# A transformer block and a ConvNeXt block on one core: q and k computed in pairs of tiles with seven block products instead of eight

## The chip, the core and the metric

The program runs on one core of a Trainium2 chip. The core has five engines, each with its own queue of instructions that are begun in order: TensorE (PE in the profile; PEld is its weight load) multiplies matrices into PSUM, VectorE (DVE) and ScalarE (ACT) work element by element, GpSimd (POOL) and SyncE (SP) are used here to start transfers. Engines wait for each other through semaphores. The metric is the time of one execution on the device in microseconds (us), as a median of several executions.

## The reference, cut to what matters

The input x is eight images of 384 channels by 32x32 pixels, in float32. Two layers follow each other: attention with an MLP, and a 7x7 depthwise convolution with an MLP that has a global response norm. In the kernel every 128x128 block of weights times 512 pixels is one TensorE product.

```python
# layer 0 (per image: N = 1024 tokens, C = 384 channels, 8 heads of 48)
xn  = layernorm(xf, g1, beta1)
qkv = einsum('bnc,oc->bno', xn, w_qkv) + b_qkv          # q, k, v
attn = softmax(einsum('bhnd,bhmd->bhnm', q, k) * SCALE)
out = einsum('bhnm,bhmd->bhnd', attn, v)
x1  = einsum('bnc,oc->bno', out, w_proj) + b_proj + xf
h   = gelu(einsum('bnc,oc->bno', layernorm(x1, g2, beta2), w_fc1) + b_fc1)
y   = x1 + einsum('bnh,oh->bno', h, w_fc2) + b_fc2
# layer 1
z = layernorm(depthwise_conv7x7(y) + dw_b) * ln_w + ln_b
z = gelu(einsum('bhwc,cd->bhwd', z, w1) + b1)
z = grn_gamma * (z * nx) + grn_beta + z                 # nx: over all pixels of an image
out = y + einsum('bhwd,dc->bhwc', z, w2) + b2
```

## The kernel before: the parts that the change and the prediction touch

The kernel is software-pipelined over the images. While TensorE works on one image's attention and MLP, VectorE does the convolution of the image before it. In the steady part TensorE's order per image is: w1 (of the image before the last), v of the new image, w2, q/k, attention, proj, fc1, fc2.

A small clock in the program, `flow`, decides where side work is placed in the order of instructions. It counts the time of the TensorE products already recorded, and a side chain says with `yield us` after how much of it the next piece is to be recorded.

```python
U = 0.857                       # one 128x128x512 product, for the clock
ps_s = ...tile_pool(name="ps_s", bufs=2, space=PSUM)    # [P, 1024] each: two banks
ps_o = ...tile_pool(name="ps_o", bufs=4, space=PSUM)    # [P, 512] each: one bank
ring = ...tile_pool(name="ring", bufs=9)                # weights, loaded up to 9 tiles ahead

def qk(b, xn):                  # q and k of one image: six output tiles m, i
    big = one.tile([P, HT * N], F32, tag="big", name=f"qk_{b}")
    parts = big[:, : 2 * NP * N].rearrange("p (i m n) -> p i m n", i=2, m=NP)
    for m in range(CT):                                 # CT = 3
        for i in range(2):                              # q, k
            ...
            def evict(dst, ps):
                nc.scalar.activation(dst, ps, AF.Identity, bias=bqk[:, at : at + 1], scale=1.0 if i else SCALE)
            args = lambda k: wqk_sb[:, k, at, :], lambda k: xn[:, k, :], CT
            if (m, i) != (CT - 1, 1):
                evict(parts[:, i, m, :], linear(*args, f"qk_{b}_{at}"))   # 3 x 2 products
    ...
    def last_tile():            # the sixth tile, called behind the first two score tiles
        for h in range(2):
            evict(parts[:, 1, CT - 1, half(h)], linear_half(*args, h, f"qk_{b}_last_{h}"))
        ...

# attention: 64 steps; each has one score tile, one exp, and the product of two steps before
for n in range(len(steps) + 2):
    if n == 2:
        last_tile()
    if n < len(steps):
        ps[n] = scores(*steps[n])         # PE s, then nc.scalar.activation(p, s, AF.Exp)
    if n >= 2:
        product(*steps[n - 2], ps.pop(n - 2))           # PE o
    ...
```

The MLP of layer 1 (w1) already uses the scheme that the change brings to q/k. Two output tiles (rows) and the first two input tiles are a 2x2 block of weights, the two halves of the pixels a 2x2 block of input, and seven products with sums of blocks take the place of eight; the third input tile takes four more, plainly. The sums of weights (s1 to s4) are made once, the differences of inputs (t1 to t4) per image by `block_differences`, in the buffer `attn`.

```python
def block_differences(acc):
    ...
    yield 3.0
    for dst, one_, other in ((t1, b12, b11), (t2, b22, t1), (t3, b22, b12), (t4, b21, t2)):
        nc.vector.tensor_tensor(dst, one_, other, ALU.subtract)
        yield 1.2

def grn_up(...):                # w1, for each of six pairs
            nc.scalar.copy(c21, product((a11, b11)))
            ...
            plus(c11, product((a13, b31), (a12, b21)), c21)    # plus: a VectorE addition, L982
            accumulate(p5, [(s1, t1)])
            plus(c21, product((s2, t2)), c21)
            plus(c12, p5, c21)
            plus(c12, product((s4, b22), (a13, b32)), c12)
            ...
            plus(c21, product((s3, t3)), c21)
            plus(c22, p5, c21)
            plus(c21, product((a23, b31), (a22, t4)), c21)
            plus(c22, product((a23, b32)), c22)
```

w2 (`o_p` in the profile, `kept` is its result) ends with two VectorE operations on its last product:

```python
    p = product(d)
    op(c11, p, c11)             # L787 kept<-o_p
    done(0, 0)
    op(c21, p, c21)             # L787 kept<-o_p
    done(1, 0)
```

The convolution is 49 taps for each of three channel tiles. VectorE does 42 of them (L911, `acc<-pad,vec,acc`), ScalarE multiplies for the other seven in halves (L932, `tap`) and GpSimd's queue adds those by transfers (L933). In the last image what is left of the convolution is recorded at once before the last convolution begins (`wqkv<-pad,vec,wqkv`).

```python
def convolution(acc, us, slow=0, ...):
    ...
            yield 2.43 if n <= CT * slow else us

start_conv(b, 1.65)             # image 0
start_conv(b, 1.8, 10)          # other images: 30 taps every 2.43 us, then every 1.8 us

def next_values(b):
    if b < B:
        flow.finish(state["norm1"])
        values(b, state["xn"])  # v
```

Of the kernel before, what the change touches and what calls it, by code (L numbers as in the profile page):

```python
# [46 lines left out]
F32 = mybir.dt.float32  # L47
AF = mybir.ActivationFunctionType
ALU = mybir.AluOpType
# [102 lines left out]
def block_kernel(  # L152
# [26 lines left out]
    quiet = []  # L179
    s_fc2 = dram.tile([P, len(FORMS), 4 * P], F32, tag="s_fc2", bufs=1, name="s_fc2")  # L180
    s_w2 = dram.tile([P, len(FORMS), 4 * P], F32, tag="s_w2", bufs=1, name="s_w2")
    s_w1 = dram.tile([P, HT // 2, 4, P], F32, tag="s_w1", bufs=1, name="s_w1")

    def half(h):
# [121 lines left out]
    def plan_thirds(name, w, sums):  # L306
        plan = []
        for i, form in enumerate(FORMS):
            plain = form[0] == "a"
            plan.append(((name, i), block_of(w, int(form[1]), int(form[2])) if plain else sums[:, i, :]))  # L310
        return plan

    def plan_fc2_fast(tag):
        return plan_thirds(f"fc2_{tag}", wfc2, s_fc2)

    def plan_w1(tag, fast=True):
        plan = []
# [169 lines left out]
            other = 64 * (i % 2) + HD  # L487
            yield at(NP - 1)[own : own + 16], at(i // 2)[other : other + 16]

    def qk(b, xn):  # L490

        big = one.tile([P, HT * N], F32, tag="big", name=f"qk_{b}")
        parts = big[:, : 2 * NP * N].rearrange("p (i m n) -> p i m n", i=2, m=NP)
        for m in range(CT):
            for i in range(2):
                at = i * CT + m

                def evict(dst, ps):
                    nc.scalar.activation(dst, ps, AF.Identity, bias=bqk[:, at : at + 1], scale=1.0 if i else SCALE)  # L499

                args = lambda k: wqk_sb[:, k, at, :], lambda k: xn[:, k, :], CT
                if (m, i) != (CT - 1, 1):
                    evict(parts[:, i, m, :], linear(*args, f"qk_{b}_{at}"))
        moves = [(own, other) for i in range(2) for own, other in pieces(lambda m: parts[:, i, m, :])]
        for own, other in moves[:-2]:
            nc.sync.dma_start(out=own, in_=other)

        def last_tile():

            for h in range(2):  # L510
                evict(parts[:, 1, CT - 1, half(h)], linear_half(*args, h, f"qk_{b}_last_{h}"))
            for own, other in moves[-2:]:
                nc.sync.dma_start(out=own, in_=other)

        return parts[:, 0], parts[:, 1], last_tile

    def heads(t):
# [369 lines left out]
        nc.sync.dma_start(out=kept.rearrange("(c p) n -> p c n", p=P), in_=xt)  # L887
        return kept

    def convolution(acc, us, slow=0, y0=0, y1=H, ready=tuple(range(CT)), taken=None):  # L890

        done = [0] * CT
        ct, n = None, 0
        taps = KS * KS - (HELPED if taken is not None else 0)
        while min(done) < taps:
            left = [c for c in ready if done[c] < taps and not (taken and taken.get(c, 0) > flow.now)]
            if not left:
                yield 1.0  # L900
                continue
            ct = min([c for c in left if c != ct] or left, key=lambda c: done[c])
            i = done[ct]
            dy, dx = divmod(i, KS)
            window = pad[:, ct, dy + y0 : dy + y1, dx : dx + W]
            dst = image(acc[:, ct, :])[:, y0:y1, :]
            tap = col("dww", ct * KS * KS + i)
            if i == 0:
                nc.vector.tensor_scalar(dst, window, tap, col("dwb", ct), ALU.mult, ALU.add)
            else:  # L910
                nc.vector.scalar_tensor_tensor(dst, window, tap, dst, ALU.mult, ALU.add)  # L911
            done[ct] += 1
            n += 1
            yield 2.43 if n <= CT * slow else us

    def help_convolution(acc, us, taken):

# [274 lines left out]
    def prepare(weights, aside):  # L1192
# [120 lines left out]
        if aside:  # L1313
            yield from shift_through_w1()
            return
        yield from forms("fc2", wfc2, s_fc2)
        weights.release()
        t = blocks("w1_sums")
        tiles = w1.rearrange("p (i a o) -> p i a o", a=6, o=P)
# [22 lines left out]
    def main():  # L1342
# [14 lines left out]
        nc.gpsimd.memset(high, 1.0)  # L1357
        make_identity(nc, ident)
        xt = load_x(0, "x", engine=nc.gpsimd)
        plan = plan_fc1(0) + plan_fc2_fast(0)  # L1360
        for b in range(1, B):
            if b < B - 1:
                plan += plan_fc1(b) + plan_fc2_fast(b)
            else:
                for h in range(2):
                    plan += plan_fc1(f"{b}_{h}") + plan_fc2(f"{b}_{h}")
            plan += plan_w1(b - 1, b < B - 1)
            if b == B - 1:
                plan += plan_w1(f"{b}_0", False)
            plan += plan_w2(b - 1, b < B - 1)  # L1370
        plan += plan_w1(f"{B - 1}_1", False) + plan_w1(f"{B - 1}_2", False)
        plan += plan_w2(f"{B - 2}_b", False)[4:] + plan_w2(B - 1, False)
        weights = Weights(plan, "fc2_0")
# [10 lines left out]
        state = {"help": None, "xn": xn, "conv": None, "acc": None, "norm1": None, "norm3": None}  # L1384
        kept = {}

        def start_conv(b, us, slow=0):
            acc = state["acc"] = one.tile([P, CT, N], F32, tag="acc", name=f"acc_{b}")
            taken = {}
            state["conv"] = flow.spawn(convolution(acc, us, slow, taken=taken), paced=True)  # L1390
            state["help"] = flow.spawn(help_convolution(acc, 2.7, taken), paced=True)

        def conv_norm(b, ln):
# [21 lines left out]
        def next_values(b):  # L1415

            if b < B:
                flow.finish(state["norm1"])
                values(b, state["xn"])

# [7 lines left out]
        def last_convolution(h, ct, ln=None):  # L1430
            if ct < 0:
                conv_norm(B - 1, ln)
                next_norms(B - 1)
                return
            ready[h].append(ct)
            if ct == 0:
                rows = (LAST[0].stop // W, H) if h else (0, LAST[0].stop // W)
                conv = convolution(last, 0.86 if h else 0.66, 0, *rows, ready[h])
                state["conv"] = flow.spawn(after(state["conv"], conv), paced=True)
                if h == 0:  # L1440
                    state["norm_a"] = flow.spawn(after(state["conv"], last_norm(LAST[0], 2.6)))

        for b in range(B):
            if b == 0:
                folding = flow.spawn(after(None, folds(weights), 8))
                preparing = flow.spawn(after(None, prepare(weights, False), 4))
                aside = flow.spawn(after(folding, prepare(weights, True), 4))
            qT, kT, last_tile = qk(b, state["xn"])
            ln2, rest, xn = attention(b, xt, qT, kT, last_tile, (folding, aside) if b == 0 else ())
            if b < B - 1:  # L1450
                mlp(b, xt, xn, weights, b, ln2, rest, lambda: next_norms(b), lambda ln: conv_norm(b, ln))
            else:
                acc = state["acc"]
                mlp_by_halves(b, xt, xn, weights, ln2, rest, last_convolution)
            kept[b] = keep(b, xt)
            if b + 1 < B:
                acc = state["acc"]
            if b == 0:
                xt = load_x(b + 1, "x")
                flow.finish(preparing)  # L1460
                start_conv(b, 1.65)
                next_values(1)
                continue
            if b < B - 1:
                xt = load_kept(b - 1, kept.pop(b - 1))
            flow.finish(state["norm3"])
            if b < B - 1:
                y, gx = grn_up(b - 1, acc, weights, b - 1)
                start_conv(b, 1.8, 10)
                scale = flow.spawn(grn_scale(b - 1, gx, weights, b - 1, y))  # L1470
                next_values(b + 1)
                flow.finish(scale)
                quiet.append("w2")
                grn_down(b - 1, y, xt, weights, b - 1, b - 1)
                quiet.clear()
                xt = load_x(b + 1, "x")
            else:

                norm_b = flow.spawn(after(state["conv"], last_norm(LAST[1], 1.0)))
                norm_c = flow.spawn(after(norm_b, last_norm(LAST[2], 1.2)))  # L1480
                y, gx = grn_up_straight(b - 1, acc, weights, b - 1)
                scale = flow.spawn(grn_scale(b - 1, gx, weights, b - 1))
                flow.finish(state["norm_a"])
                sums = small.tile([P, CT, HT], F32, tag="gx_last", bufs=1, name="gx_last")
                y_last = places()
                last_up(last, y_last, 0, sums, weights)
                flow.finish(scale)
                halves = lambda k, part: y[:, k, part]
                blocks = [(r, half(n)) for r in range(CT) for n in range(2)]
                args = b - 1, halves, kept[b - 1], weights  # L1490
                grn_down_straight(*args, b - 1, b - 1, blocks[:-1])
# [147 lines left out]
```

## Time and profile before

| what | value |
|---|---|
| time, median of three | 3334.23 us (3333.64 to 3336.33) |
| span of the profiled execution | 3332.5 us, granted TensorE clock 0.996 |
| one image in the steady part | 403.5 to 404.1 us |
| VectorE busy in such an image | 303 us |
| ScalarE busy in such an image | 202 us |
| TensorE busy, all | 3298.9 us |
| q/k products: `qk` and `qk_last`, records | 480 and 96 |

The page of the profile gives the busy time of each engine, and the costliest groups of instructions as line, engine, operation, output<-input, shape and count, with the busy time and the mean of one in ns. A float32 matmul has two records, each with a weight load. The chain of waits follows the work that ended last, as start, duration and what; its counts include weight loads. The timeline has start, duration, engine, line and operation, with the idle time ahead of it and what ended it in brackets.

### The profile page before, as it was taken

The numbers are of one execution on the slowest core, as the hardware profiler recorded it, in microseconds if no ns is written. First come the engines' busy times: TensorE is split into PE (matmuls) and PEld (weight loads), VectorE is DVE, ScalarE is ACT, GpSimd is POOL, SyncE is SP. The second block draws the span as 40 slices with busy tenths as digits, with TensorE's granted clock in tenths as the row PEclk, the third lists the DMA queues.
The fourth block names the chain that finished last, engine by engine and source line by source line (L and its number), as shares of the span: only waits on it lengthen the run. The fifth ranks groups of instructions, "written<-read, shape, count | busy, mean of one in ns | idle before, by whom it ended". The sixth has DMA issues, their size and how long they took to land.

```text
span 3332.5 us, 38500 instructions
## 1 busy us (share of the span) xinstructions
PE 3298.9 (99%) x14338; PEld 1418.3 (43%) x14338; DVE 2387.2 (72%) x2986; ACT 1593.0 (48%) x2180; POOL 480.9 (14%) x565
## 2 busy tenths in 40 slices
PE   8999999999999999999999999999999999999998
PEld 4344434443344433444344443444434444344455
DVE  4445786787857878579785797767886678879950
ACT  2542663346634375353652636526374355623541
POOL 2121210112110121101111022110220112200000
PEclk9999999999999999999999999999999999999999
DMA  5336632656335653537426374263742647423231
GB/s 186 111 108 149 138 68 67 157 121 134 59 92 138 139 114 58 122 112 167 83 54 142 104 176 71 50 166 92 172 76 54 177 93 158 74 72 89 64 99 44
DMA packets 195828, 362.43 MB, mean 109 GB/s; under 512 B 40368, under 2 KB 46384, under 8 KB 195248
## 3 DMA queue, kind: packets, MB, share of 16 engines
q0 software_dynamic: 80640, 157.85, 26.2%
q1 hardware_dynamic: 114704, 201.32, 19.9%
q8 instruction: 116, 1.90, 0.2%
q10 hardware_dynamic: 288, 0.71, 0.1%
q14 instruction: 80, 0.66, 0.1%
HBM read 181.52 MB, written 33.82 MB: 65 GB/s over the span
## 4 chain that ended last, share of the span: by engine, by line
PE 82%; DVE 6%; issue 2%; ACT 0%; DMA 0%; SPq 0%; POOL 0%; DVEq 0%; POOLq 0%
PE s L597 11%; PE o L617 11%; PE fc L347 10%; PE h L354 10%; PE fc_p L354 10%; PE o_p L354 9%; PE qk L334 5%; DVE wqkv L911 4%; PE o L1037 4%; PE v L525 3%; PE proj L539 3%; PE h_last L1081 2%; PE qk_last L347 1%; DVE acc L911 1%; PE ln_sum L390 1%
## 5 line engine op out<-in xcount | busy, mean ns | idle before, releaser
L911 DVE SCALAR_TENSOR_TENSOR acc<-pad,vec,acc 128x1024 f32<-128x1024 f32 x861 | 1061.0, 1276 | 27.8 <-DMA acc<-tap 24.0
L606 ACT ACTIVATE p<-s 128x1024 f32<-128x1024 f32 x512 | 523.2, 1023 | 271.7 <-PE s L597 262.2
L597 PE MATMUL s<-qk 48*64 48x512 f32 x4096 | 546.6, 592 | 1.5 <-ACT qk L499 1.5
L617 PE MATMUL o<-p,v 64*64 64x512 f32 x4096 | 542.4, 590 | 0.0
L347 PE MATMUL fc<-xn,fc 128*128 128x512 f32 x1152 | 502.3, 594 | 0.0
L933 POOL DMA_DIRECT2D acc<-tap x294 | 254.2, 870 | 1164.3 <-ACT tap L932 735.1
L347 PEld LDWEIGHTS fc<-xn,fc 128*128 128x128 f32 x1152 | 217.9, 190 | 280.2 <-issue 268.1
L354 PE MATMUL fc_p<-hid,fc 128*128 128x512 f32 x728 | 317.7, 593 | 0.0
L366 ACT ACTIVATE hid<-fc,bfc_f 128x512 f32<-128x512 f32 x192 | 131.4, 686 | 348.2 <-PE fc L347 348.1
L617 PEld LDWEIGHTS o<-p,v 64*64 64x64 f32 x4096 | 162.8, 133 | 281.4 <-issue 274.5
L597 PEld LDWEIGHTS s<-qk 48*64 48x64 f32 x4096 | 158.5, 133 | 283.8 <-issue 225.3
L354 PE MATMUL o_p<-y,w 128*128 128x512 f32 x624 | 270.9, 593 | 0.0
L982 DVE TENSOR_TENSOR y<-h,y 128x512 f32<-128x512 f32 x288 | 196.8, 690 | 91.4 <-PE h L354 76.2
L354 PEld LDWEIGHTS fc_p<-hid,fc 128*128 128x128 f32 x728 | 138.0, 190 | 176.2 <-issue 171.7
L932 ACT ACTIVATE tap<-pad,vec 128x512 f32<-128x512 f32 x294 | 210.3, 724 | 1.8 <-DMA acc<-tap 1.8
L334 PE MATMUL qk<-xn,wqkv 128*128 128x512 f32 x480 | 207.4, 593 | 0.0
L354 PE MATMUL h<-acc,w_A 128*128 128x512 f32 x432 | 207.3, 595 | 0.0
L911 DVE SCALAR_TENSOR_TENSOR wqkv<-pad,vec,wqkv 128x416 f32<-128x416 f32 (+1 forms) x288 | 193.5, 747 | 0.5
L354 PEld LDWEIGHTS o_p<-y,w 128*128 128x128 f32 x624 | 118.2, 190 | 148.5 <-issue 133.3
L558 DVE TENSOR_TENSOR attn<-o,attn 128x512 f32<-128x512 f32 x64 | 44.2, 690 | 181.9 <-ACT attn L556 181.1
L721 ACT COPY pad<-x 128x512 f32<-128x512 f32 x48 | 30.2, 635 | 251.9 <-DVE x L787 193.9
L334 PEld LDWEIGHTS qk<-xn,wqkv 128*128 128x128 f32 x480 | 91.2, 190 | 114.0 <-issue 111.9
(294 smaller groups left out, 3544.7 us busy)
## 6 DMA issues: line engine op xcount, KB each, us to landing
acc<-tap POOLq DMA_DIRECT2D x294, 256.0 KB, 3.4
w_A<-in_w SPq DMA_DIRECT2D x72, 384.0 KB, 3.2
fc<-s_fc SPq DMA_DIRECT2D x91, 256.0 KB, 2.9
hid<-hid POOLq DMA_DIRECT2D x42, 512.0 KB, 7.5
fc<-in_wfc SPq DMA_DIRECT2D x54, 384.0 KB, 5.8
w<-s_w SPq DMA_DIRECT2D x78, 256.0 KB, 2.7
y<-y POOLq DMA_DIRECT2D x36, 512.0 KB, 6.9
kept<-x SPq DMA_DIRECT2D x8, 1536.0 KB, 8.2
```

Source lines behind the costliest of these rows:

```text
L334: nc.tensor.matmul(out=ps[:, half(h)], lhsT=lhsT(k), rhs=rhs(k)[:, half(h)], start=(k == 0), stop=(k == nk - 1),)
L347: nc.tensor.matmul(out=ps, lhsT=lhsT(k), rhs=rhs(k)[:, half(h)], start=(k == 0), stop=(k == nk - 1))
L354: nc.tensor.matmul(out=bank, lhsT=lhsT, rhs=rhs, start=k == 0, stop=k == len(pairs) - 1)
L366: nc.scalar.activation(dst, src, function, **kw)
L597: nc.tensor.matmul(out=s[64 * i : 64 * i + 64, j, :], lhsT=kT[64 * j : 64 * j + HD, m, k0 : k0 + 64], rhs=qT[64 * j : 64 * j + HD, m, half ...
L606: nc.scalar.activation(p, s, AF.Exp)
L617: nc.tensor.matmul(out=outs[i][64 * j : 64 * j + 64, :], lhsT=v[keys, t, at : at + 64], rhs=p[keys, j, :], start=(t == 0), stop=(t == KT - 1),
L911: nc.vector.scalar_tensor_tensor(dst, window, tap, dst, ALU.mult, ALU.add)
L932: nc.scalar.mul(t.rearrange("p (h w) -> p h w", w=W), window, tap)
L933: nc.gpsimd.dma_start(out=acc[:, ct, half(h)], in_=t, accum_op=ALU.add)
L982: nc.vector.tensor_tensor(dst, bank, part, ALU.add)
L1037: nc.tensor.matmul(out=ps, lhsT=tiles[k], rhs=y(k, part), start=(k == 0), stop=(k == HT - 1))
```

## The change: what it does, and what it is for

Images 1 to 7 compute q and k by pairs: the q tile m and the k tile m are the two output rows of a 2x2 block, as in w1. So a pair takes eleven products instead of twelve. This is for less work on TensorE. In exchange:

- the sums of weights `s_qk` are made once in image 0, kept in DRAM, and loaded per image through the ring (three tiles);
- the differences of xn are made during the v products, behind w1 (their buffer `attn` is then free) and well ahead of q/k;
- the parts of a pair are put together by eight VectorE additions and a ScalarE copy, and ScalarE then applies bias and scale in SBUF;
- the third pair stands behind the first two score tiles, where the last k tile alone stood;
- the taps of the convolution are spaced wider during q/k (every 4.4 us) and a little closer elsewhere.

Image 0 keeps the plain products.

```diff
-    def qk(b, xn):
+    def qk(b, xn, weights=None):
 ...
+        def finish(i, m, src, cols=slice(0, N)):
+            at = i * CT + m
+            bias = bqk[:, at : at + 1]
+            nc.scalar.activation(parts[:, i, m, cols], src, AF.Identity, bias=bias, scale=1.0 if i else SCALE)
 ...
+        def fast(m):
+            b11, b12, b21, b22, b31, b32 = (xn[:, s, half(n)] for s in range(CT) for n in range(2))
+            t1, t2, t3, t4 = (attn[:, i, :] for i in range(4))
+            a11, a12, a13, _, a22, a23 = (wqk_sb[:, k, i * CT + m, :] for i in range(2) for k in range(CT))
+            sums = weights.at(f"qk_{b}", m)
+            s1, s2, s3, s4 = (sums[:, k, :] for k in range(4))
+            c11, c12, c21, c22 = (parts[:, i, m, half(n)] for i in range(2) for n in range(2))
+            if m < CT - 1:
+                p5 = ps_s.tile([P, 2, NH], F32, tag="s", name=f"qk_{b}_{m}_5")[:, 0, :]
+            else:
+                p5 = o_tile(f"qk_{b}_{m}_5")
 ...
+            nc.scalar.copy(c21, product((a11, b11)))
+            plus(c11, product((a13, b31), (a12, b21)), c21)
+            accumulate(p5, [(s1, t1)])
+            plus(c21, product((s2, t2)), c21)
+            plus(c12, p5, c21)
+            plus(c12, product((s4, b22), (a13, b32)), c12)
+            finish(0, m, parts[:, 0, m, :])
+            move(0, m)
+            plus(c21, product((s3, t3)), c21)
+            plus(c22, p5, c21)
+            plus(c21, product((a23, b31), (a22, t4)), c21)
+            plus(c22, product((a23, b32)), c22)
+            weights.used(f"qk_{b}", m)
+            finish(1, m, parts[:, 1, m, :])
+            move(1, m)
+
+        def last_tile():
+            if weights:
+                fast(CT - 1)
+                return
 ...
+            yield next((early for m, early in first if n <= m), us)
-            yield 2.43 if n <= CT * slow else us
 ...
+        t = one.tile([P, CT, N], F32, tag="acc", name="qk_sums").rearrange("p c n -> p (c n)")
 ...
+        add(t[:, 0], a21, a22)
+        sub(t[:, 1], t[:, 0], a11)
+        sub(t[:, 2], a11, a21)
+        sub(t[:, 3], a12, t[:, 1])
+        for j in range(4):
+            nc.gpsimd.dma_start(out=s_qk[:, :, j * P : (j + 1) * P], in_=t[:, j])
 ...
                 flow.finish(state["norm1"])
+                differences = flow.spawn(block_differences(state["xn"]))
                 values(b, state["xn"])
+                flow.finish(differences)
 ...
-            qT, kT, last_tile = qk(b, state["xn"])
+            qT, kT, last_tile = qk(b, state["xn"], weights if b else None)
 ...
-                start_conv(b, 1.65)
+                start_conv(b, 1.6, (9, 1.65), (17, 4.4))
 ...
-                start_conv(b, 1.8, 10)
+                start_conv(b, 1.8, (28, 2.43), (36, 4.4))
```

## The prediction

> **What bounds the kernel now.** I read the busy row first, then the chain of waits through one image in the steady part (image 3, from 1154 us), then the timelines of VectorE and ScalarE over the same stretch, and last the end of the program.
>
> ```profile
> PE 3298.9 (99%) x14338; PEld 1418.3 (43%) x14338; DVE 2387.2 (72%) x2986; ACT 1593.0 (48%) x2180; POOL 480.9 (14%) x565
> 1102.76 51.53 PE o_p L354 x120
> 1154.29 25.77 PE qk L334 x60
> 1180.05 0.02 issue
> 1180.08 1.12 ACT qk L499
> 1181.20 0.04 issue
> 1181.24 1.09 PE s L597 x8
> 1182.33 5.35 PE qk_last L347 x12
> 1187.68 1.02 PE s L597 x8
> ```
>
> TensorE is busy 99% and the chain runs through it alone, so a product removed is time removed, unless something new makes TensorE wait. A 128x128x512 product stands as two records, each with its weight load: x60 is 30 products in 25.77 us, 0.859 us each. One wait is visible: the second score tile stands behind a 1.12 us eviction of q/k on ScalarE.
>
> ```profile
> 1155.79 2.48 DVE L911 SCALAR_TENSOR_TENSOR acc<-pad,vec,acc 128x1024 f32<-128x1024 f32 x2
> 1158.18 0.69 DVE L787 TENSOR_TENSOR kept<-o_p,kept 128x512 f32<-128x512 f32 x1
> 1158.78 1.28 DVE L911 SCALAR_TENSOR_TENSOR acc<-pad,vec,acc 128x1024 f32<-128x1024 f32 x1
> 1159.97 1.28 DVE L787 TENSOR_TENSOR kept<-o_p,kept 128x512 f32<-128x512 f32 x2
> 1161.17 26.89 DVE L911 SCALAR_TENSOR_TENSOR acc<-pad,vec,acc 128x1024 f32<-128x1024 f32 x22
> 1181.21 1.28 ACT L362 ACT_TABLE_LOAD   x1
> 1182.50 1.94 ACT L606 ACTIVATE p<-s 128x1024 f32<-128x1024 f32 x2
> ```
>
> VectorE enters q/k late: the last sums of w2 (kept<-o_p) end at 1161.2, 7 us after q/k began on TensorE. Today this is harmless, as q/k asks nothing of VectorE; it does 22 convolution taps in a row, 1.22 us each. ScalarE loads a table and then does two exponentials.
>
> ```profile
> 2956.29 9.20 DVE L911 SCALAR_TENSOR_TENSOR acc<-pad,vec,acc 128x1024 f32<-128x1024 f32 x7
> 2972.02 0.75 DVE L725 SCALAR_TENSOR_TENSOR x<-fc,vec,x 128x512 f32<-128x512 f32 x1 [1.87 <-PE fc L347]
> 3131.03 18.72 PE L1081 MATMUL h_last<-wqkv,w_A 128*128 128x416 f32 x48 [2.42 <-DVE gmean L1098]
> ```
>
> In the last image VectorE does the seven taps left of one convolution at 2956, starts the last convolution at 2974 after only 1.87 us of rest, and works without a gap until TensorE waits for it at 3131. There, lateness of VectorE is lateness of the program.
>
> **What the Trainium skill says.** "VectorE: DVE Perf Modes", section "The TRN2 errata", gives (N+151)/0.96 ns for an fp32 addition of two tensors, 691 ns at 512; the same kind of addition in w1 (y<-h,y) has a mean of 690 ns, so it agrees, and I use 0.69 for the new additions. "ScalarE: Activation LUTs", section "What ACT_TABLE_LOAD costs", gives about 1283 ns; the line above has 1.28 us. "PSUM — Partial Sum Buffer", section "Specifications (TRN2)", gives eight banks of 2 KiB; the kernel's pools use all of them (two pairs, four single), so a product soon has to wait for the reader of an older one. The trace shows such waits only as a hint: the weight load of q/k waited 0.3 us for kept.
>
> **The change part by part.**
>
> *Removed.* A pair of q and k tiles took 12 products, now 11 (seven for the 2x2 blocks, four for the third input tile). Three pairs in images 1 to 7: 21 products x 0.859 = 18.0 us. The ACT wait before the second score tile (about 1.15 us, seven times, 8 us) also goes, because the third pair now stands behind both score tiles and these need the first pair only. Ceiling: 26 us, so 3308.
>
> *Added.* Per image 24 VectorE additions (24 x 0.69 = 16.6 us) and four differences (2.8 us), three ScalarE copies (1.7 us); three loads of 256 KB, early in the ring of nine. In the instruction order of the changed kernel eight taps stand among the additions instead of 22 behind them. VectorE has 16.6 + 8 x 1.2 = 26 us of work in q/k, TensorE 28.4. That would fit, did VectorE not start late.
>
> *The stage walked through, images 2 to 7.* Zero is the first q/k product (1154.29). The order and waits of the built program say which bank each product takes. Without waits a pair's eight groups end at 0.9, 2.6, 3.4, 4.3, 6.0, 6.9, 8.6 and 9.45.
> 1. VectorE finishes w2 at 6.95 (1161.25) and has a tap in front of the first addition: 8.1.
> 2. The sixth group takes the bank of w2's last product: wanted at 6.0, free at 7.0, wait 1.0. The seventh takes the bank of the first addition: wanted 7.9, free 8.8, wait 0.9. Pair 1's first product needs a bank that VectorE leaves at 12.0, wanted 11.4: 0.7.
> 3. VectorE from 8.1: 16 additions and four taps (11.0 + 4.8), and about 0.6 for a ScalarE copy that itself stands behind the finishing of k. The last addition of pair 1 ends at about 24.2.
> 4. ScalarE, in its order: finish k of pair 1 (1.1), table (1.28), a tap (0.7), two exponentials (1.9), and only then the copy of pair 2's first product (0.6): 29.8. TensorE wants that bank at 27.5: wait 2.3.
> 5. VectorE again, from 29.8: eight additions and two taps, 37.5. ScalarE: finish 1.1, tap 0.7, exponential 1.0: 40.3. The fifth score tile needs this exponential's buffer and was ready at 38.3: wait 2.0.
>
> Sum: 33 x 0.859 = 28.4, six half steps of 0.86 = 5.2, waits 6.9: the fifth score tile starts at 40.4. Before it started at 1191.28, that is 37.0. So each of six images loses about 3.4 us: +20.
>
> *Image 1* has the v products ahead of q/k, VectorE about 1 us late, and no table load (the trace goes from the eviction to the exponential directly). The same walk gives one wait of 0.7 and a start of 34.2: -2.8.
>
> *The end.* In the new order the bulk of taps in the last image is 13, not seven: +6 x 1.2 = 7.2 us, against 1.87 us of rest: the last convolution starts 5.3 us later relative to TensorE, and VectorE sets the end: +5.
>
> *Elsewhere.* The other convolutions end about 10 to 20 us later in the program's order; in image 3 VectorE rests 15.5 and 13.6 us around the following norm, so this costs nothing. In image 1 VectorE is nearly full: 0 to 2 us. The weight sums of image 0 are four additions of 128x384 beside TensorE's work: about 0.
>
> Total: 3334 + 20 - 3 + 5 = 3356.
>
> **The rivals.** *TensorE keeps the gain.* The same scheme runs in w1 already, where 66 products take 57.06 us, 0.865 each, so banks can keep up. For it: four banks give slack and one or two of my waits may overlap. Against: w1 has no taps between its additions and no late start. It would make 3308 to 3320. *Waits cancel the gain.* If only the late start counts (2.6 us) and ScalarE keeps up, each image saves about 1 us and the end takes most of it back: 3328 to 3335. *VectorE becomes the bound of the whole image.* Its busy time goes from 303 to about 320 of 404 us; gaps in attention take this, but if taps pile up before fc2 its sums come late as well, a few us per image: 3365 to 3380.
>
> **Range and chances.** The walk says 3356. I shade it to 3352, since overlaps can only take waits away and the first rival is real, about one in eight. The low end, 3322, lets each wait be half of mine and the end cost nothing; the high end, 3366, adds 1.5 us per image. 2% is 67 us, far beyond the ceiling of 26 and beyond any wait I see: faster 0.01, within 2% 0.97, slower 0.02.
>
> **What would show it.** Right, if TensorE has 42 matmul records fewer than before, and gaps of 5 to 8 us in total between the last o_p record and the fifth score tile, put down to VectorE's qk additions and to ScalarE; if the fifth score tile starts near 40 us after q/k begins in images 2 to 7 and near 34 in image 1; and if TensorE's wait for the last gmean stays. Wrong, if the stage is gapless and ends before 36, or if VectorE's late entry has gone. A loss outside q/k and the last image would mean a term that I have not got.

## The result and the profile after

The changed kernel takes 3364.96 us (median, 3364.1 to 3366.96), the kernel before 3334.22: a ratio of 1.0092, with a 95% interval of 1.0074 to 1.0109. It is slower by 31 us, inside the range and 13 us above the predicted 3352; the walk itself had said 3356.

The first product of q/k in each image is a good milestone, as the stages between two of them are the same in all runs. From those starts and the spans of the two profiles (3332.5 and 3362.3 us):

| from one q/k start to the next (us) | before | after | difference | predicted |
|---|---|---|---|---|
| image 0 | 309.9 | 315.6 | +5.7 | about 0 |
| image 1 | 403.9 | 401.0 | -2.9 | -2.8 |
| images 2 to 6, five together | 2018.4 | 2036.4 | +18.0 | +17 |
| image 7, to the end | 563.6 | 573.3 | +9.7 | +3.4 +5 |

Line numbers from here on are those of each kernel printed; in the changed one L967 is the taps, L358 the products by single banks, L536 q/k's additions, L538 ScalarE's copy, L653 and L662 the scores and exponentials, L843 the sums of w2. The busy row of the page after, to be read against that of before (14338 products, 2387.2 us of VectorE):

```profile
PE 3284.5 (98%) x14296; PEld 1418.9 (42%) x14296; DVE 2515.5 (75%) x3186; ACT 1603.1 (48%) x2194; POOL 484.2 (14%) x569
```

The 42 records are gone and TensorE works 14.4 us less, yet the span is 30 us longer: what was lost is waiting. TensorE's waits after, with what released it, the sum, the number and the longest:

```profile
PE qk L358 <- ACT qk L538: 10.6, 6, 1.8
PE s L653 <- ACT p L662: 8.6, 6, 1.4
PE qk L358 <- DVE qk L536: 6.8, 12, 0.7
PE fc L351 <- DVE acc L423: 6.1, 1, 6.1
PE qk L358 <- DVE kept L843: 6.0, 6, 1.0
...
PE b L247 <- DVE w_gbeta L1363: 2.9, 1, 2.9
PE b L247 <- issue: 2.3, 1, 2.3
...
PE h_last L1137 <- DVE gmean L1154: 0.4, 1, 0.4
```

None of the lines with qk in front stood in the list of before; each comes six times (12 is two for each image), for images 2 to 7. The two lines with b are image 0, the line with fc is the last image. In image 3, where TensorE's timeline of before has one rest of 0.18 us in q/k, it now has five (the last column is the idle time and its releaser):

```profile
1166.89 1.13 PE L358 MATMUL qk<-attn,qk 128*128 128x512 f32 x2 [1.00 <-DVE kept L843]
1168.68 1.12 PE L358 MATMUL qk<-xn,wqkv 128*128 128x512 f32 x2 [0.67 <-DVE qk L536]
...
1171.99 2.84 PE L358 MATMUL qk<-xn,wqkv 128*128 128x512 f32 x6 [0.47 <-DVE qk L536]
...
1189.83 1.12 PE L358 MATMUL qk<-xn,qk 128*128 128x512 f32 x2 [1.76 <-ACT qk L538]
...
1200.29 1.09 PE L653 MATMUL s<-qk 48*64 48x512 f32 x8 [1.43 <-ACT p L662]
```

q/k began at 1159.72, so the fifth score tile stands at 40.6 instead of 37.0. VectorE's timeline shows why the first rests come: when TensorE is 8 us into q/k, VectorE still has w2's sums (kept<-o_p) and a tap in front of the first addition.

```profile
1165.56 1.28 DVE L843 TENSOR_TENSOR kept<-o_p,kept 128x512 f32<-128x512 f32 x2
1166.75 1.27 DVE L967 SCALAR_TENSOR_TENSOR acc<-pad,vec,acc 128x1024 f32<-128x1024 f32 x1
1167.95 2.20 DVE L536 TENSOR_TENSOR qk<-qk,qk 128x512 f32<-128x512 f32 x3
```

In the last image VectorE has 13 taps in bulk instead of 7, and the first sum of the last convolution (x<-fc) has no rest in front of it any more; it stands 215.7 us after q/k (2789.04), before 203.1:

```profile
2983.08 17.14 DVE L967 SCALAR_TENSOR_TENSOR acc<-pad,vec,acc 128x1024 f32<-128x1024 f32 x13 [1.70 <-DMA acc<-tap]
...
3004.78 0.75 DVE L781 SCALAR_TENSOR_TENSOR x<-fc,vec,x 128x512 f32<-128x512 f32 x1
```

TensorE then waits in a new place, before fc1's second half, and hardly at all for the last gmean:

```profile
3026.88 17.78 PE L351 MATMUL fc<-xn,fc 128*128 128x512 f32 x36 [6.07 <-DVE acc L423]
...
3164.13 14.93 PE L1137 MATMUL h_last<-wqkv,w_A 128*128 128x416 f32 x42 [0.38 <-DVE gmean L1154]
```

### The profile page after: what moved, and what is told of

Its sections match the earlier page's. It is cut to its first block, busy times and chain, and to the rows that moved or that the text cites. A ratio compares the mean times of both kernels' runs of the same rounds, so it can differ in the third digit from the quotient of the medians.

```text
span 3362.3 us, 38774 instructions
## 1 busy us (share of the span) xinstructions
PE 3284.5 (98%) x14296; PEld 1418.9 (42%) x14296; DVE 2515.5 (75%) x3186; ACT 1603.1 (48%) x2194; POOL 484.2 (14%) x569
## 5 line engine op out<-in xcount | busy, mean ns | idle before, releaser
L967 DVE SCALAR_TENSOR_TENSOR acc<-pad,vec,acc 128x1024 f32<-128x1024 f32 x861 | 1069.2, 1275 | 10.2 <-DMA acc<-tap 5.3
L662 ACT ACTIVATE p<-s 128x1024 f32<-128x1024 f32 x512 | 522.6, 1024 | 273.3 <-PE s L653 266.3
L653 PE MATMUL s<-qk 48*64 48x512 f32 x4096 | 546.9, 592 | 8.8 <-ACT p L662 8.6
L358 PE MATMUL fc_p<-hid,fc 128*128 128x512 f32 x728 | 319.2, 594 | 0.0
L653 PEld LDWEIGHTS s<-qk 48*64 48x64 f32 x4096 | 164.0, 133 | 285.0 <-issue 213.9
L358 PE MATMUL o_p<-y,w 128*128 128x512 f32 x624 | 270.9, 592 | 0.0
L358 PEld LDWEIGHTS fc_p<-hid,fc 128*128 128x128 f32 x728 | 137.2, 190 | 178.5 <-issue 172.4
L358 PE MATMUL h<-acc,w_A 128*128 128x512 f32 x432 | 207.3, 596 | 0.0
L967 DVE SCALAR_TENSOR_TENSOR wqkv<-pad,vec,wqkv 128x416 f32<-128x416 f32 (+1 forms) x288 | 193.5, 742 | 0.5
L358 PEld LDWEIGHTS o_p<-y,w 128*128 128x128 f32 x624 | 118.0, 190 | 148.7 <-issue 133.5
L536 DVE TENSOR_TENSOR qk<-qk,qk 128x512 f32<-128x512 f32 x168 | 112.5, 687 | 48.4 <-ACT qk L538 40.9
L358 PE MATMUL qk<-xn,wqkv 128*128 128x512 f32 x252 | 123.7, 600 | 6.8 <-DVE qk L536 6.8
```

What stands on the lines that cost most here:

```text
L358: nc.tensor.matmul(out=bank, lhsT=lhsT, rhs=rhs, start=k == 0, stop=k == len(pairs) - 1)
L536: nc.vector.tensor_tensor(dst, bank, part, ALU.add)
L653: nc.tensor.matmul(out=s[64 * i : 64 * i + 64, j, :], lhsT=kT[64 * j : 64 * j + HD, m, k0 : k0 + 64], rhs=qT[64 * j : 64 * j + HD, m, half ...
```

## The experiments

Theory A is the prediction's: TensorE loses in q/k because VectorE enters late and ScalarE's order puts other work ahead of a copy, both felt through four single banks; beside that image 0 and the end lose a few us each. Theory B: VectorE's load (303 us before, 320 after, of some 404 an image) is the loss, wherever it falls. Theory C: eleven products and 24 additions cannot run through these banks without waits. All runs but the last two change the changed kernel in one respect. Each was timed beside the kernel before on the same chip (3333.3 to 3334.1 us there).

**1. Plain q/k.** All pairs by plain products; sums, differences and the new taps stay.

```
-            qT, kT, last_tile = qk(b, state["xn"], weights if b else None)
+            qT, kT, last_tile = qk(b, state["xn"], None)
```

> q and k of images 1 to 7 by plain products again, six tiles with three input tiles each; the making of the weight sums in image 0, the differences of xn and the new spacing of VectorE's taps stay as in the changed kernel. Theory A (the loss in images 2 to 7 is TensorE's waits inside q/k, which come from VectorE's late entry and ScalarE's order; beside it 5 us in image 0, where VectorE stands at the weight sums, and 5 us at the end from the six more taps in bulk): these two remain, 3334 + 5 + 5 = 3344, between 3341 and 3348. Theory B (VectorE's larger load, 303 to 320 us an image, is the loss wherever it falls): the 24 additions are gone, so 3334 to 3338. Theory C (seven products cannot keep their gain because of the banks): as A here.

Measured 3337.35 us, ratio 1.0009 (1.0001 to 1.0018). Theory A's number was too high, and B's range has it; but the parts are A's: image 0 is 315.1 us (+5.2) and the last image 566.9 (+3.3), without a single fast pair. What A missed is that images 1 to 6 are 0.3 to 1.6 us shorter than before (402.6 for most of 403.6). That gain lies outside q/k (the fifth score tile stands at 37.0 in both). In image 4 it lies in the sums of the convolution's norm: before, TensorE made the two sets of 64x64 products one after the other, 2.04 us from the first start to the next fc product (1768.67 to 1770.71); here they start in pairs 0.01 us apart and take 1.02 (1780.45 to 1781.47). Which part of the change brings that about was not tested. So 27.6 us hang on the fast pairs, and this run alone does not tell A from B.

**2. The table load ahead of q/k.**

```
+        if weights:
+            ln_table()
         big = one.tile([P, HT * N], F32, tag="big", name=f"qk_{b}")
```

> The changed kernel with one move: ScalarE's load of the exponential's table stands ahead of q/k, where ScalarE has little to do, not between the finishing of pair 1's k tile and the two exponentials. Theory A: the copy of pair 2's first product comes 1.3 us earlier, TensorE's wait for it falls from 1.76 to about 0.5 and the wait of the fifth score tile may shrink too: 1.3 to 2 us less in each of six images, 3353 to 3357. Theory B (VectorE's load sets the stage, ScalarE only seems to): VectorE's additions then hold TensorE instead, 3362 to 3365.

Measured 3355.93 us, 1.0065 (1.0052 to 1.0079): 9 us less, as A has it. The wait for ScalarE's copy fell from 10.6 us in six to 2.0; the other waits in q/k stayed. ScalarE's order was a real term.

```profile
PE qk L358 <- ACT qk L540: 2.0, 6, 0.3
```

**3. A pause of the taps, dense taps afterwards.**

```
-                start_conv(b, 1.8, (28, 2.43), (36, 4.4))
+                start_conv(b, 1.4, (22, 2.43), (23, 44.0))
```

> The changed kernel with no convolution tap on VectorE from the last third of w2 to the end of q/k: 22 taps at 2.43 us, a pause of 44 us, the rest 1.4 us apart, so that about as many taps as before (14 against 13) stand in bulk at the end. Nothing else is changed; VectorE does the same work. Theory A: VectorE enters q/k with its w2 sums done and keeps up, the waits of 1.0, 0.67, 0.47, 1.76 and 1.43 us go, the fifth score tile starts about 35 us after q/k: 32 us less in six images, 3331 to 3340. Theory B (VectorE's load is the loss wherever it falls): the taps that leave q/k delay attention or the norm instead, 3355 to 3365. Theory C (with single banks for eleven products the additions are always waited for): at least 3 us an image stay, 3350 or more.

Measured 3353.83 us, 1.0057 (1.0043 to 1.0071). By the number alone A has failed. TensorE's timeline of image 3 says otherwise for q/k: no rest, and the fifth score tile at 34.3 us. The time went in attention, where taps 1.4 us apart make a multiplication late for proj (the reciprocal that it needs, by way of a transfer, stands 158.7 us after q/k with taps on both sides, against 151.7 in run 5):

```profile
1320.54 1.88 PE L595 MATMUL proj<-attn,wproj_sb 128*128 128x512 f32 x4
1324.50 7.97 PE L595 MATMUL proj<-attn,wproj_sb 128*128 128x512 f32 x14 [2.08 <-DVE attn L640]
```

This wait comes in five of the images, 11.0 us in all. And 14 records take 7.97 us here, where 13 took 5.74 before. The windows around it give the reason in the column after POOL, the granted clock of TensorE:

```profile
1322.00:1324.50 2.50, 0.42 (x1) 0.00 (x0) 0.74 (x2) 0.00 (x0) 0.00 (x0) 1.00 0.21 67
1324.50:1328.00 3.50, 3.50 (x4) 1.48 (x5) 1.27 (x5) 0.00 (x0) 0.00 (x0) 0.51 0.00 0
```

After the 2.08 us pause the clock stood at 0.51 for 3.5 us, another 1.7 us lost; this came in three of the five images. A score tile in attention also waits 0.8 to 1.5 us for an exponential in each of the five. Together that is some 22 of the 26 us by which the five images are longer than in run 5; the rest I did not place. C falls with this run, although the time is in its range, as the seven-product scheme ran through the banks without a rest; the spacing of 1.4 us, not the scheme, took the gain back (run 5 has the same pause without it).

**4. Image 0.** A pause ahead of the weight sums.

```
         yield from forms("fc2", wfc2, s_fc2)
+        yield 6.0
         t = one.tile([P, CT, N], F32, tag="acc", name="qk_sums").rearrange("p c n -> p (c n)")
```

> The changed kernel with 6 us of pause in image 0 ahead of the four additions that make the weight sums of q and k, so that VectorE does other work until the stores of the fc2 forms have left the buffer, instead of standing there for 3 us in front of the first norm's sums. Theory A: image 0 loses 5 us because of that stand, so 3358 to 3361.5. Theory B (the added transfers and their place in the chain of preparations cost it, not the stand): the rest of the preparations comes 6 us later and the time stays, 3363 to 3368.

Measured 3359.34 us, 1.008 (1.0066 to 1.0093), image 0 at 309.4 us, so A holds. TensorE's waits for b fall from 6.4 us to 0.5. In the changed kernel VectorE stood here for the stores of the fc2 forms, whose buffer the sums take, with the sums for TensorE's b (w_lnb) queued behind:

```profile
98.23 1.42 DVE L1281 TENSOR_TENSOR fc_b<-fc_b 128x512 f32<-128x512 f32 x2
102.67 0.56 DVE L1281 TENSOR_TENSOR qk_sums<-wqkv 128x384 f32<-128x384 f32 x1 [3.02 <-DMA s_fc<-fc_b]
```

**5. The pause again, without dense taps.** Images 2 to 6 only.

```
-                start_conv(b, 1.8, (28, 2.43), (36, 4.4))
+                start_conv(b, 1.8, *(((28, 2.43), (36, 4.4)) if b == B - 2 else ((22, 2.43), (23, 44.0))))
```

> The pause of VectorE's taps again (none from the last third of w2 to the end of q/k), but with the spacing of 1.8 us afterwards that the changed kernel has, and only in images 2 to 6: the last image keeps the changed kernel's taps. The taps that leave q/k go to the bulk at the end of a convolution, 19 instead of 13, where VectorE rests 22 us afterwards. Theory A (late entry through the single banks; in the run with 1.4 us it was the dense taps in attention that took back the gain, by a late multiplication in front of proj and a lower granted clock after that wait): the fifth score tile at about 34.3 us after q/k, an image in 401 us instead of 407, five images 6.2 us shorter each: 3332 to 3337. Theory B (VectorE's load is the loss wherever it falls): some other wait on VectorE stands in for them, 3350 or more.

Measured 3329.98 us, 0.999 (0.9984 to 0.9997): 35 us less than the changed kernel and 2 below A's range. The five images take 400.5 to 401.2 us instead of 407 to 408, and TensorE has no rest in q/k. VectorE does the same work as in the changed kernel and is now the one that waits (here in image 3, q/k from 1154.40):

```profile
1154.60 1.29 DVE L843 TENSOR_TENSOR kept<-o_p,kept 128x512 f32<-128x512 f32 x2 [0.25 <-PE o_p L358]
1157.23 0.69 DVE L536 TENSOR_TENSOR qk<-qk,qk 128x512 f32<-128x512 f32 x1 [1.34 <-ACT tap L988]
1158.89 1.42 DVE L536 TENSOR_TENSOR qk<-qk,qk 128x512 f32<-128x512 f32 x2 [0.97 <-PE qk L358]
...
1179.73 4.33 DVE L536 TENSOR_TENSOR qk<-qk,qk 128x512 f32<-128x512 f32 x6 [5.55 <-ACT qk L538]
```

This settles images 2 to 6: the loss was when VectorE worked, not how much, so B falls there. The last line also shows ScalarE's copy still behind table and exponentials, with 5.55 us for VectorE and none for TensorE: once VectorE is on time, the order on ScalarE costs next to nothing (the fifth score tile stands at 34.25 us, and at 34.05 in run 8, which also moves the table load). The two terms of the walk were not independent.

**6. The third pair ahead of the first scores.** fast(m) for all three pairs in the loop, nothing left in last_tile.

```
             if weights:
-                if m < CT - 1:
-                    fast(m)
+                fast(m)
                 continue
```

> The changed kernel with the third pair of q and k ahead of the first scores, all else alike. Theory A (standing behind the first scores hides the finishing of the pairs; the table load and two exponentials in front of a copy are its smaller price): the waits of 1.76 and 1.43 us go, but now the first exponential follows the last finishing and the table load, the third score tile waits about 4 us for it and the fifth starts at about 43 us: 2 to 3 us more in each of six images and 4 in image 1, 3377 to 3390. Theory D (the place behind the first scores is what went wrong): 3 us less an image, 3346 to 3352.

Measured 3386.06 us, 1.0162 (1.0148 to 1.0175). A's sum and its wait:

```profile
1194.71 1.95 PE L651 MATMUL s<-qk 48*64 48x512 f32 x16
1200.83 1.67 PE L651 MATMUL s<-qk 48*64 48x512 f32 x8 [4.17 <-ACT p L660]
```

The third score tile waits 4.17 us for the first exponential and the fifth stands at 43.5 us. Image 1 lost 1.3 us up to that tile, not 4. The third pair's place is worth 21 us to the changed kernel. (The clock was 0.56 for 3.2 us after this pause as well.)

**7. The old taps in the last image only.**

```
-                start_conv(b, 1.8, (28, 2.43), (36, 4.4))
+                start_conv(b, 1.8, *(((30, 2.43),) if b == B - 2 else ((28, 2.43), (36, 4.4))))
```

> The changed kernel with the old spacing of the taps (30 at 2.43 us, then 1.8) in the last of the convolutions only, the one that runs in image 7: 8 taps in bulk instead of 13. Theory A (the later bulk makes VectorE late in the last image: TensorE waits 6.1 us for the norm in front of fc1's second half and runs at a granted clock of 0.75 for 10 us after that; 2 us of the former wait for the last gmean are gone instead): the end gets 4 to 6 us shorter, against 1 to 3 us more of waits in q/k of that image, 3360 to 3363. Theory B (the last image is long by VectorE's additions alone): 3365 to 3368.

Measured 3368.66 us, 1.0107 (1.0091 to 1.0122): 4 us more than the changed kernel and 0.7 above B's range, so A falls for the end. The bulk has 7 taps again and TensorE's 6.07 us before fc1 are gone; from the fifth score tile to the end it is 529.8 us for 532.7. But q/k has more and longer waits (2.89 us for one score tile), and that tile stands at 47.6 instead of 40.6. The first sum of the last convolution stands at 216.0 us after q/k, against 215.7:

```profile
3004.89 0.75 DVE L781 SCALAR_TENSOR_TENSOR x<-fc,vec,x 128x512 f32<-128x512 f32 x1
```

Here moved taps only changed the place where time is lost. That suggested theory E: in the last image VectorE is the bound, and its additions cost time in whatever order.

**8. All mendings.** Edits 2 and 4, the pause of edit 5 in images 2 to 6, and the taps of edit 7 in the last image.

> All mendings in one: the pause of the taps in images 2 to 6, the old spacing in the last image, the table load ahead of q/k, and the 6 us of pause ahead of the weight sums in image 0. The seven-product scheme and the third pair behind the first scores stay. Theory A: image 0 as before the change, image 1 2.9 us and images 2 to 6 2.7 us shorter than before the change, the last image about even: 3334 - 2.9 - 13.7 = 3318, between 3314 and 3326, faster than both kernels. Theory B (VectorE's load) or C (the banks): 3334 or more.

Measured 3326.36 us, 0.998 (0.9972 to 0.9988), 0.4 us above A's range. Images 1 to 6 take 400.3 to 400.9 us each and image 0 310.1, but the last 575.0 where I had assumed 563.6.

**9. All mendings, the last image plain.** No fast pairs and no differences of xn there (36 products instead of 33).

```
-            qT, kT, last_tile = qk(b, state["xn"], weights if b else None)
+            qT, kT, last_tile = qk(b, state["xn"], weights if 0 < b < B - 1 else None)
```

> The kernel with all mendings, and q and k of the last image by plain products again (eighteen instead of sixteen and a half for each half of them, no additions, no differences of its xn). Theory E (in the last image VectorE is the bound up to the first layer of the last convolution block: that layer began 375 us after q/k in the changed kernel and in both runs that changed the taps there, against 362 before, wherever TensorE's wait stood): it begins at 362 again, the last image takes 563.6 us instead of 575.0, and the whole 3313 to 3318. Theory A alone (only the order of the taps and the late entry make the last image longer): 3 to 4 us come back from q/k there, 3322 to 3324.

Measured 3314.96 us (3312.76 to 3315.57), 0.9941 (0.9927 to 0.9955): faster than both kernels, by 19 and 50 us. The first sum is back at 202.7 us after q/k (2748.27), with its rest, and h_last at 361.7:

```profile
2951.00 0.75 DVE L783 SCALAR_TENSOR_TENSOR x<-fc,vec,x 128x512 f32<-128x512 f32 x1 [1.88 <-PE fc L351]
```

The last image takes 564.4 us. From the first sum to h_last it is 159 us in the kernel before, in the changed one and in runs 7 and 9, VectorE being busy 156 of them (TensorE 153 to 157); the stretch ahead of it has 172 us of VectorE's work in the changed kernel and in run 7, 157 in the other two. The stretch ahead, from the first q/k product to the first sum, in run 7 and in run 9 (length, then PE, PEld and DVE busy):

```profile
2788.90:3005.00 216.10, 205.55 (x1245) 83.36 (x1244) 171.79 (x194) 118.45 (x146) 37.23 (x44) 0.98 0.46 97
2748.30:2951.00 202.70, 202.41 (x1250) 81.74 (x1249) 156.97 (x170) 116.69 (x143) 37.23 (x44) 1.00 0.47 97
```

With the taps of runs 7 to 9, E's numbers hold: without the 15 us of VectorE's work the first sum comes 13 us earlier and the last image is 10.6 us shorter than in run 8. That the additions cost time in whatever order is not shown. Order moves the first sum too: run 1 has 157 us of work ahead of it and reaches it at 209.8 us, run 3, whose taps pause in the last image as well, has 173 and reaches it at 211.7, with a last image of 569.2 us. VectorE is idle for 38 to 53 us ahead of the first sum in all these runs. So a better order for fast pairs in the last image stays open; none that was tried brought it below 569.2.

## Why the prediction was right, and where not

**Images 2 to 7, q/k: right.** All five waits stand where the walk put them, with the releasers that it named: 1.00, 0.67, 0.47, 1.76 and 1.43 us for its 1.0, 0.9, 0.7, 2.3 and 2.0. That view counts from the modelled end of a record; by the starts of the records the gaps are 1.2, 0.9, 0.6, 1.9 and 1.6, 6.2 us in all for the predicted 6.9. The fifth score tile stood at 40.6 us, predicted 40.4. That it is so close is partly luck: the walk had 33.6 us of products without waits, where run 5 takes 34.25, so two errors of about 0.7 us cancel (its sums are also rounded: 8.1 + 11.0 + 4.8 + 0.6 is 24.5, not 24.2). Run 5 shows the cause by taking it away: 6.1 to 7.2 us an image.

**Image 1: right in the number**, a start at 34.1 for 34.2, and -2.9 us for -2.8. The one wait of 0.7 us in it did not come; some 0.5 us more of products than the walk had made up for it.

**Image 0: wrong.** "The weight sums of image 0 are four additions of 128x384 beside TensorE's work: about 0." The additions do take only 2.2 us; the 5.7 come from the buffer they were put into (run 4). This one term is most of the distance between the walk's 3356 and the result. It is the "term that I have not got"; a smaller one is a wait of 0.4 to 1.0 us for ln_sq in images 2 to 6, in fc1.

**The end: right in size, wrong in its way.** "The last convolution starts 5.3 us later relative to TensorE, and VectorE sets the end: +5", with 3.4 of q/k before it, was 8.4 us; 9.7 came. Its start moved by 12.6 us and not by 8.7. Of that, run 1 shows 6.7 by the taps alone (209.8 for 203.1), the rest comes with the additions. I had counted the displaced taps and not that the additions displace VectorE's time as well, in the one image where VectorE sets the end. Some was given back: at the product that waits for the last gmean the delay is 13.0 us, at the end 9.7. That wait shrank from 2.42 to 0.38 us, as TensorE's pause of 6.07 us stood before fc1, and the half clock that followed it before (1.7 us lost) did not come; the other 1.6 us I did not place. "If TensorE's wait for the last gmean stays" was thus a wrong sign to look for.

**Removed: 18.0 us was right; "about 1.15 us, seven times, 8 us" of ScalarE's wait was not.** The waits list of before has 1.5 us for all eight of these. The chain named the eviction, 1.12 us long, but most of it lay beside TensorE's own last product. The ceiling was nearer 19.5 than 26 us. (Run 9 gains 3.3 us an image in 2 to 6; 2.9 of them are q/k's, 34.05 for 37.0, and the rest lies outside it, as in run 1.) The total did not suffer, since the walk started from the measured 37.0.

**The rivals.** "VectorE becomes the bound of the whole image" came near the truth in the last image alone. "Waits cancel the gain" needed a ScalarE that keeps up; its copies and exponentials held TensorE for 10.6 and 8.6 us. "TensorE keeps the gain" is what the scheme can do: 400.3 us an image for 403.6.

## What to carry to other kernels

When a change gives the evicting engine new work in a stage, ask first when that engine enters the stage: here the same change cost 3.5 us an image with VectorE 8 us late and saved 3 us with its optional work paused beforehand. Optional work did least harm where the engine rests afterwards (22 us at the bulk of images 2 to 6 in the changed kernel). A change that pays in the steady part can cost in a stage where this engine has no such rest: leaving it out of the last image gave 10.6 us. A small preparation needs a free buffer as much as a free engine.

## What the runs showed of the hardware

A short pause can cost TensorE more than its own length. After pauses of 2.08 (run 3), 2.89 (run 7), 4.17 (run 6) and 6.07 us (the changed kernel) the granted clock stood at 0.50 to 0.57 for about 3 to 4 us. After the 2.42 us in front of the last gmean of the kernel before it was 0.57 as well. Two windows of the changed kernel, the first right behind its pause of 6.07 us, show the step back:

```profile
3026.90:3030.90 4.00, 4.00 (x5) 1.79 (x6) 4.00 (x8) 2.29 (x4) 0.00 (x0) 0.50 0.00 0
3030.90:3035.00 4.10, 4.10 (x10) 1.71 (x9) 3.40 (x6) 2.38 (x3) 0.00 (x0) 0.98 0.36 96
```

After 1.76 us in image 3 it stayed at 1.00, and after 2.10 and 2.48 us in run 8 too. But in run 7 a pause of 1.70 us, up to 2814.70, was followed by 0.51 from 2816.4 to 2819.9, and in image 4 of run 4 two pauses of 1.00 and 0.67 us, up to 1568.37 and 1570.16, by 0.55 from 1570.1 to 1573.9. So the length of one pause does not decide; what else does was not tested. The Trainium skill, "TensorE: Matmul & The Clock Gate", section "HAM oscillation — how this bites in real kernels", names gaps over about 3.4 us as the ones to avoid; here the half clock agrees with that page, but pauses of 1.70 and 2.08 us were enough, and the measurement decides.
